# Graph output bias as a per-partition scalar of the self-feature sum, value copies on ScalarE, and another place for one group's condition features

## Chip, cores and metric

The kernel runs on one core of a Trainium2 chip. The time is the device time of one execution in microseconds. Before the change the median of three runs is 674.63 us (674.51 to 674.78).

A core has a matrix engine (TensorE, PE in the profile, with its weight loads listed as PEld), a vector engine (VectorE, DVE), an engine for activation functions and scaled copies (ScalarE, ACT), a general engine (GpSimd, POOL) and a queue that issues most transfers (SyncE, SP). Each executes its own instructions in order and waits on semaphores for the others. Transfers between HBM and the core's SBUF run on 16 DMA engines. PE writes to PSUM, which VectorE and ScalarE read; GpSimd works on SBUF alone.

## The reference, cut to what matters

64 batches of 64 tokens with 256 features. A graph attention over the first 20 tokens of each batch, in two directions with 16 heads, is followed by a transformer block with adaptive layer norms. The change touches only the graph attention. Cut to its core:

```python
row_zero = v.sum(-1) == 0
q_exp = where(row_zero[..., None], 0, q[:, None, :])
self_feat = concat([v, q_exp], -1) @ W_self.T + b_self
output = self_feat
for d in range(2):
    A = adj_f if d == 0 else swapaxes(adj_f, 1, 2)
    A = A[:, :, :20, :]
    cond = A.sum(-1);  vb = A @ w_bias + b_bias
    kv = self_feat[:, :20]
    aff = qh @ kh * 0.25                      # 16 heads
    aff = where(cond > 0, aff, NEG) + vb
    w = softmax(aff, -1)
    out = einsum('bnhf,hgf->bnhg', w @ kv, Wout[d]) + bout[d]
    output = output + out
x = v + relu(output)
# then: layer norm, 16-head attention, gated residual, layer norm, gelu MLP, gated residual
```

Since the softmax weights of a row sum to 1, adding `bout` to the values before the weighting gives the same sum as adding it to the output after it. Over the two directions the second form adds `bout[0] + bout[1]`, which depends on the feature alone.

## The kernel before, in words

**Layout.** Everything is kept transposed: features on the 128 partitions in two halves c = 0, 1, tokens along the free dimension. The batches are cut into nine groups (`NB`): group 0 of 4 batches (256 tokens), groups 1 to 7 of 8 batches (512 tokens), group 8 of 4. A tile is 128 tokens, two batches; a group has two or four tiles, numbered j.

**Order.** The schedule is written out by hand; each engine executes in the order in which the Python code emits. `start()` brings group 0 through the graph stage and prepares groups 1 and 2. Then for g = 1 to 7 come `boundary(g)` and `period(g)`; `finish()` does the rest. In a period each *slot* (`slot`, L763) works on one tile E of group g in the transformer block and one tile C of group g+1 in the graph stage: scores of both, `block_turned` and `graph_turned` for the tiles of the slot before (`Eb`, `Cb`), keys for the next slot, `block_exp(E)`, `graph_masked(C)`, `block_sums(E)`, `graph_exp(C)`, `block_weights(E)`, `block_attended(Eb)`, `graph_output` for each of `Cb`, `graph_normal(C)`. Between these stand named places ("p", "p2", "f0", "f1", "d0", "d0b", "f2", "f2a", "f2b", "d1", "d2", "f3") that `fill` fills with work of other groups: MLP products of group g-1 (`mlp_up` L735, `mlp_down` L745), features and masks of group g+2. `start()` ends with two slots for the tiles (0, 0), (0, 1) of the block and (1, 2), (1, 3) of the graph stage; the first of them has `Cb` = the tiles 0 and 1 of group 1 and the flag `late`, by which `graph_exp(C)` and `block_weights(E)` stand behind the two `graph_output`.

**PSUM.** `pair` gives the two score buffers "pa" and "pb"; `bank` hands out four others in rotation, so a product can only start when the reader of what last stood in its bank is done.

**Self features.** `self_product` (L324) multiplies x with W_self; `self_cond` makes `tq`, the conditioning masked by the rows that are not zero; `self_features` (L331) adds the product, `b_self` and `tq` on VectorE and GpSimd copies the first 20 tokens to `kv`. For groups 0 to 2 `self_cond` reads the row sums from PSUM on VectorE (L309). From group 3 on `nonzero_rows` sums the rows of x on VectorE (L288), compares (L291), and SP writes the 512 flags to DRAM (`nzd`, L293), element by element, and reads them back spread over the partitions (`nzb`, L294); `self_cond` is then a GpSimd product (L315), one for each half c. For group 3 `nonzero_rows` is called in `boundary(1)`, and both `self_cond` stand in "f1" of slot 0 of period 1, behind `graph_masked(C)`; for later groups they stand in "d2".

**Masks.** `load_adj` loads two tables of 440 KB into the two buffers `a_d`; `mask_step` reduces them on VectorE to `keep` and `term` (L347 to L360). The tables of group 3 are loaded in `boundary(1)` ahead of `nonzero_rows(3)` and read from slot 1 of period 1 on.

**Values.** `graph_v` multiplies `kv` with Wout (L371 for the first 128 rows, L382 for the other 32), adds the bias on VectorE into `v_sb` (L373 with `bout_sb`, L387 with `bout4`), and SP writes that to DRAM, from where `graph_v_spread` (L395) brings it into `vblk` in the form that `graph_output` needs. `bout_sb` and `bout4` are filled at the start by five broadcasting transfers (L149, L151) between the loads of wq and those of group 1.

**Scores to output.** `graph_masked`: VectorE multiplies the scores by `keep` (L469), GpSimd adds `term` (L474). `graph_exp`: VectorE takes the maximum (L479) and subtracts it (L480), ScalarE takes the exponent (L481). `graph_normal`: L486, L487 on VectorE, L488 on GpSimd. `graph_turned` transposes on PE (L496), copies on ScalarE (L500). `graph_output` multiplies with the values (L514) into `po`. For the tiles of group 0 and tiles 0 and 1 of group 1 (`early`) PE also adds the self features by an identity product (L510) and ScalarE takes the Relu out of PSUM (L521); for all others VectorE adds (L523) and ScalarE takes the Relu (L524). GpSimd adds the result to x (L525). Each fp32 product shows as two matmuls in the profile.

**Block stage.** `block_exp` (L629, L631 on VectorE, L635 on ScalarE), `block_sums` (L639), `block_weights` (L642 on VectorE, L643 on GpSimd), `block_turned` (L654 on PE, L657 on ScalarE), `block_attended` (L665, L675). ScalarE has to load an activation table between Exp and Gelu (the table loads under L635 and L737).

Of the kernel before, what the change touches and what calls it, by code (L numbers as in the profile page):

```python
# [9 lines left out]
F32 = mybir.dt.float32  # L10
I32 = mybir.dt.int32
AF = mybir.ActivationFunctionType
# [5 lines left out]
P = 128  # L18
# [15 lines left out]
_COLS = [  # L34
    ("b_self", 2), ("bq0", 2), ("bq1", 2), ("bk0", 2), ("bk1", 2),
    ("bq", 2), ("bk", 2), ("bv", 2), ("bproj", 2), ("b1", 8), ("b2", 2), ("bt", 12),
    ("g1", 2), ("be1", 2), ("g2", 2), ("be2", 2),
]
COL = {}
NCOL = 0  # L40
# [6 lines left out]
def graph_attention_then_dit_block(  # L47
# [11 lines left out]
    wq: bass.AP,  # L59
    wk: bass.AP,  # L60
    wout: bass.AP,
    bout: bass.AP,
    wqkv: bass.AP,
    wproj: bass.AP,
    w1: bass.AP,
# [77 lines left out]
    wk_sb = [load_w(f"wk{d}", wk[d], 2, D, nc.sync) for d in range(2)]  # L143
    load_adj(0)
    wq_sb = [load_w(f"wq{d}", wq[d], 2, D, nc.sync) for d in range(2)]
    bout_sb = const.tile([P, 2 * D], F32, name="bout_sb")

    bout4 = const.tile([P, P], F32, name="bout4")
    nc.sync.dma_start(bout_sb, bout.partition_broadcast(P))  # L149
    for i in range(4):  # L150
        nc.sync.dma_start(bout4[ts(i, 32), :], bout[ts(i, P)].partition_broadcast(32))  # L151
    load_xT(1)
    wout_sb = load_w("wout", wout, 2, 2 * D, nc.sync)
    wb = const.tile([P, L], F32, name="wb")
# [44 lines left out]
    nc.gpsimd.tensor_tensor(hmask2, hmask4[:, 0:2], hmask4[:, 2:4], ALU.add)  # L199
    mhalf = const.tile([P, 2], F32, name="mhalf")  # L200
    nc.gpsimd.memset(mhalf, -0.5)

    vblk = const.tile([4 * M, GB, 2, HD, 8], F32, name="vblk")

# [158 lines left out]
    def graph_v(g, part):  # L363

        G = groups[g]
        if part == 0:
            n = min(G.nb * M, P)
            G.vd = dram.tile([GB * M, 2 * D], F32, tag="vd", name="vd")[0 : G.nb * M, :]
            pv = bank("pv")[0:n, :]
            for k in range(2):  # L370
                nc.tensor.matmul(pv, G.kv[:, k, 0:n], wout_sb[:, k, :], start=(k == 0), stop=(k == 1))  # L371
            v_sb = small.tile([P, 2 * D], F32, tag="v_sb", name="v_sb", bufs=1)[0:n, :]
            nc.vector.tensor_tensor(v_sb, pv, bout_sb[0:n, :], ALU.add)  # L373
            nc.sync.dma_start(G.vd[0:n, :], v_sb)
            return
        if G.nb * M <= P:
            return

        pv = bank("pv4")
        for k in range(2):  # L380
            for i in range(4):
                nc.tensor.matmul(  # L382
                    pv[ts(i, 32), 0:P], G.kv[:, k, ds(P, 32)], wout_sb[:, k, ts(i, P)],
                    start=(k == 0), stop=(k == 1), tile_position=(0, 32 * i),
                )
        v4_sb = small.tile([P, P], F32, tag="v4_sb", name="v4_sb", bufs=1)
        nc.vector.tensor_tensor(v4_sb, pv[:, 0:P], bout4, ALU.add)  # L387
        for i in range(4):
            nc.sync.dma_start(G.vd[P : GB * M, ts(i, P)], v4_sb[ts(i, 32), :])

# [38 lines left out]
    def graph_keys(g, j):  # L429

        G = groups[g]
        G.kblk = getattr(G, "kblk", {})
        kblk = G.kblk[j] = two.tile([P, 2, 2, 2, 4 * M], F32, tag="kblk", name="kblk")
        if g == 1:
            for h in range(4):
                nc.scalar.activation(
                    kblk.rearrange("p d c s (h m) -> p h (d c s) m", h=4)[:, h],
                    G.kT[:, j].rearrange("p d c (s m) -> p (d c s) m", s=2), AF.Copy, scale=hmask4[:, h : h + 1],
                )
            return  # L440
        nc.gpsimd.tensor_tensor(
            kblk.rearrange("p d c s (h m) -> p (d c s) h m", h=4),
            G.kT[:, j].rearrange("p d c (s m) -> p (d c s) m", s=2).unsqueeze(2).to_broadcast([P, 8, 4, M]),
            hmask4.unsqueeze(1).unsqueeze(3).to_broadcast([P, 8, 4, M]), ALU.mult,
        )
# [56 lines left out]
    def graph_output(t, po):  # L502

        G, j = groups[t.g], t.j
        sf, xs = G.sfT[:, :, ts(j, P)], G.xT[:, :, ts(j, P)]
        po2 = po[:, 0:D].rearrange("p (c t) -> p c t", c=2)
        early = t.g == 0 or (t.g == 1 and j < 2)
        if early:
            for c in range(2):
                nc.tensor.matmul(po2[:, c], ident, sf[:, c], start=(c == 0), stop=False, skip_group_check=True)  # L510
        for c in range(2):
            for s in range(2):
                for i in range(4):
                    nc.tensor.matmul(  # L514
                        po[ts(i, 32), ds(c * P + s * N, N)],
                        vblk[:, 2 * j + s, :, :, 4 * c + i].rearrange("p h e -> p (h e)"),
                        t.wT[:, 4 * c + i, ts(s, N)], start=not early, stop=True, tile_position=(0, 32 * i),
                        skip_group_check=early,
                    )
        if early:  # L520
            nc.scalar.activation(sf, po2, AF.Relu)  # L521
        else:
            nc.vector.tensor_tensor(sf, po2, sf, ALU.add)  # L523
            nc.scalar.activation(sf, sf, AF.Relu)  # L524
        nc.gpsimd.tensor_tensor(xs, xs, sf, ALU.add)  # L525

# [236 lines left out]
    def slot(e, c, e_next, c_next, before, fill, late=False):  # L763
        Eb, Cb = before
        fill("p")
        sc = [pair("pa", "sca"), pair("pb", "scb")] if e or c else None
        E = block_scores(*e, sc) if e else None
        C = graph_scores(*c, sc) if c else None
        fill("p2")
        if Eb:  # L770
            block_turned(Eb)
        elif Cb:
            graph_turned(Cb[0])
        fill("f0")
        if e_next:
            block_keys(*e_next)
        if c_next and c_next[0] != 1:
            graph_keys(*c_next)
        if E:
            block_exp(E)  # L780
        if c_next and c_next[0] == 1:
            graph_keys(*c_next)
        if C:
            graph_masked(C)
        fill("f1")
        if Eb and Cb:
            graph_turned(Cb[0])
        if E:
            block_sums(E)
        fill("d0")  # L790
        if C and not late:
            graph_exp(C)
        fill("d0b")
        if E and not late:

            block_weights(E)
        if Eb:
            block_attended(Eb, pair("pa", "pao")[:, 0])
        fill("f2")
        for i, t in enumerate(Cb):  # L800
            if i > 0:
                graph_turned(t)
                fill("f2a")
            graph_output(t, pair("pa" if i > 0 else "pb", "po")[:, 0])
        if late:
            graph_exp(C)
            block_weights(E)
        fill("f2b")
        fill("d1")
        if C:  # L810
            graph_normal(C)
        fill("d2")
        fill("f3")
        return E, [C] if C else []

    def boundary(g, before):
# [36 lines left out]
        if a_on:  # L853
            if g > 1:
                load_x(g + 2)
            load_xT(g + 2)
            load_adj(g + 2)
        K = [Tile() for _ in range(A.nt // 2)]
        if g == NG - 2:
            pair_proj(g - 1, 0)  # L860
            norm_tokens(G, G.xT, 1)
            norm_stats(G)
            normed(G)
            pair_product(g - 1, 1)
            graph_q(g + 1, 1, 0)
            norm_tokens(K[0], A.xT, 0)
            pair_gated(g - 1, 1)
            modulated(G, G.hT, 1, amp1, off1, g)
            pair_added(g - 1, 1)
            graph_q(g + 1, 1, 1)  # L870
            graph_k(g + 1, 1)
            norm_stats(K[0])
        else:
            if Cb:
                norm_tokens(G, G.xT, 1)
                norm_stats(G)
            block_proj(g - 1, 0)
            if Cb:
                normed(G)
            block_proj(g - 1, 1)  # L880
            if c_on:
                graph_q(g + 1, 1, 0)
            if g == 1:
                graph_q(2, 1, 1)
            if Cb:
                modulated(G, G.hT, 1, amp1, off1, g)
            if not c_on:
                mlp_down(g - 2, 1, 4, 5)
            if c_on:
                graph_k(g + 1, 1)  # L890
            if g == 1:
                nonzero_rows(3)
            for j2, k in enumerate(K):
                norm_tokens(k, A.xT, j2)
                norm_stats(k)
# [59 lines left out]
    def period(g):  # L955
# [36 lines left out]
        else:  # L992
            fills = [
                {
                    "f1": [(block_v, g, i) for i in range(1 if g in (1, NG - 2) else 0, 2)] + (conds if g == 1 else []),
                    "d0": masks(0) if g > 1 else [],
                    "d2": masks(1) + conds if g > 1 else [],
                    "f3": up(0, 1, 2, 3),
# [34 lines left out]
    def start():  # L1033
# [74 lines left out]
        for t in t1:  # L1108
# [31 lines left out]
            },  # L1140
            {
                "f1": [(half_normed, 1, 1)],
                "d0b": [(half_normed, 1, 2), (graph_v, 2, 0)],
                "f2b": [(time_product, 4), (time_product, 5), (time_sum, 4), (time_sum, 5)],
            },
        ]
# [163 lines left out]
```

## Time and profile before

| what | value |
|---|---|
| median of 3 runs | 674.63 us |
| profiled execution, whole time | 675.26 us |
| its span, from the first to the last instruction | 673.6 us |
| TensorE clock granted | 1.00 throughout |
| busy: PE / PEld / DVE / ACT / POOL | 655.7 / 404.2 / 472.2 / 354.9 / 371.5 us |
| L373 and L387, the bias adds on the values | 9 of 683 ns and 7 of 282 ns |
| L523, the self-feature sum; L521, the Relu of the early tiles | 28 of 392 ns; 4 of 384 ns |
| L510, the identity products of the early tiles | 16 matmuls, 2.5 us busy |
| L315, condition features of groups 3 to 8 | 12, 12.0 us busy |
| DMA | 33.42 MB, q1 (SP) busy 15.2% of 16 engines' span |

Busy time is what an engine spent on instructions; PE's is modelled, since matmuls are pipelined. In the lists, an entry gives its start, its length, the engine, the line of the kernel, what it writes and reads, and in brackets how long the engine had idled before it and what it waited for. "SPq" is SP issuing a transfer; the transfer itself ends later. Busy times of some 97% for PE say that the other engines matter where PE waits for them.

### The profile page before, as it was taken

The page shows a single profiled execution, that of the slowest core. Times are in us where ns is not written, and L with a number is a line of the kernel's source. Part 1 is how long each engine was busy: PE and PEld are TensorE (multiplying, and loading weights), DVE is VectorE, ACT ScalarE, POOL GpSimd, SP SyncE. Part 2 cuts the span into 40 slices and gives each one's busy share as a digit, 9 for nine tenths or more (in the row PEclk, how much of TensorE's full clock was granted, in tenths as well). Part 3 has the DMA queues.
Part 4 walks back from the last instruction along what each step waited for, and adds up shares of the span by engine and source line. Part 5 has one row for each costly group of instructions (what it writes and reads, how often), then busy time and mean ns, then how long its engine had stood idle before and what let it go on. Part 6 is the DMA issues. An engine that isn't in the chain of part 4 may idle for free.

```text
span 673.6 us, 15450 instructions
## 1 busy us (share of the span) xinstructions
PE 655.7 (97%) x6422; PEld 404.2 (60%) x6422; DVE 472.2 (70%) x859; ACT 354.9 (53%) x627; POOL 371.5 (55%) x366
## 2 busy tenths in 40 slices
PE   8999898999999999999999999999999999999997
PEld 7657656775555565565555655555565675556546
DVE  4988967997777677776776777776777865656221
ACT  3364537763666337744476436654377444854412
POOL 5556557756664567653584555744667546445210
PEclk9999999999999999999999999999999999999999
DMA  7626030014100310004000140003000000000000
GB/s 239 201 87 209 27 99 18 18 34 123 18 1 34 126 31 17 18 17 156 1 18 18 36 137 17 2 32 89 10 10 11 18 26 1 2 18 1 17 16 32
DMA packets 34654, 33.42 MB, mean 50 GB/s; under 512 B 5624, under 2 KB 28408, under 8 KB 34584
## 3 DMA queue, kind: packets, MB, share of 16 engines
q1 hardware_dynamic: 34104, 32.33, 15.2%
q8 instruction: 51, 0.84, 0.6%
q14 instruction: 19, 0.16, 0.1%
q10 hardware_dynamic: 416, 0.09, 0.1%
q0 software_dynamic: 64, 0.01, 0.0%
HBM read 25.59 MB, written 6.83 MB: 48 GB/s over the span
## 4 chain that ended last, share of the span: by engine, by line
PE 84%; DVE 7%; ACT 3%; POOL 2%; issue 1%; DMA 1%; SPq 0%; ACTq 0%; POOLq 0%; DVEq 0%
PE py L745 15%; PE pu L735 15%; PE pqT L422 8%; PE pqk L580 8%; PE ppT L654 4%; PE pv L588 4%; PE pwT L496 3%; PE pf L324 3%; PE pproj L690 3%; PE po L514 3%; PE pk L407 2%; PE pao L665 2%; PE pv L371 2%; PE sca L618 2%; PE pxT L533 2%; PE phT L560 2%
## 5 line engine op out<-in xcount | busy, mean ns | idle before, releaser
L745 PE MATMUL py<-u,w 128*128 128x512 f32 (+1 forms) x272 | 117.9, 561 | 0.2 <-ACT u L737 0.2
L735 PE MATMUL pu<-h2T,w 128*128 128x512 f32 (+1 forms) x256 | 108.8, 569 | 0.9 <-POOL h2T L567 0.5
L643 POOL TENSOR_TENSOR pr<-pr,sm 128x1024 f32<-128x1024 f32 x32 | 60.9, 1903 | 69.0 <-DVE sm L642 48.3
L474 POOL TENSOR_TENSOR w<-w,term 128x640 f32<-128x640 f32 x32 | 49.5, 1550 | 72.4 <-DVE w L469 39.4
L735 PEld LDWEIGHTS pu<-h2T,w 128*128 128x128 f32 x256 | 47.7, 190 | 48.6 <-issue 43.0
L745 PEld LDWEIGHTS py<-u,w 128*128 128x128 f32 x272 | 47.8, 190 | 36.4 <-issue 32.9
L737 ACT ACTIVATE u<-pu,vec 128x512 f32<-128x512 f32 (+1 forms) x72 | 43.2, 640 | 34.3 <-PE pu L735 34.1
L422 PE MATMUL pqT<-sfT,wq 128*128 128x512 f32 (+1 forms) x144 | 60.7, 551 | 0.3 <-DVE y L713 0.3
L580 PE MATMUL pqk<-hT,wqkv 128*128 128x512 f32 (+1 forms) x144 | 59.8, 551 | 0.5 <-POOL hT L567 0.4
L629 DVE TENSOR_REDUCE mx<-sca 128x8 f32<-128x512 f32 x32 | 22.0, 689 | 50.4 <-PE sca L458 49.0
L639 DVE TENSOR_REDUCE sm<-pr 128x16 f32<-128x1024 f32 x32 | 38.9, 1217 | 21.6 <-ACT pr L635 21.3
L481 ACT ACTIVATE w<-w 128x640 f32<-128x640 f32 x32 | 23.5, 736 | 57.9 <-DVE w L480 57.9
L423 ACT ACTIVATE qT<-pqT,vec 128x512 f32<-128x512 f32 (+1 forms) x36 | 23.0, 640 | 50.9 <-PE pqT L422 50.6
L635 ACT ACTIVATE pr<-pr 128x1024 f32<-128x1024 f32 x32 | 33.8, 1057 | 26.9 <-DVE pr L631 26.6
L657 ACT COPY pT<-ppT 128x512 f32<-128x512 f32 x64 | 34.4, 591 | 25.1 <-PE ppT L654 25.1
L546 POOL TENSOR_TENSOR rstd<-rstd,mhalf 128x2 f32<-128x2 f32 x32 | 23.3, 728 | 42.1 <-DVE rstd L545 41.1
L581 ACT ACTIVATE qk<-pqk,vec 128x512 f32<-128x512 f32 (+1 forms) x36 | 23.0, 640 | 43.4 <-PE pqk L580 43.4
L488 POOL TENSOR_TENSOR w<-w,sm 128x640 f32<-128x640 f32 x32 | 44.1, 1381 | 1.9 <-DVE sm L487 1.8
L551 DVE TENSOR_SCALAR xn<-xn,mv,rstd 128x256 f32<-128x256 f32 x64 | 37.9, 633 | 9.8 <-POOL rstd L546 9.8
L542 DVE BATCH_NORM_STATS2 st<-xn 128x6 f32<-128x256 f32 x64 | 26.1, 408 | 25.5 <-ACT xn L535 25.5
L525 POOL TENSOR_TENSOR xT<-xT,sfT 128x256 f32<-128x256 f32 x32 | 23.4, 731 | 32.6 <-ACT sfT L524 27.2
L500 ACT COPY wT<-pwT 80x512 f32<-80x512 f32 x64 | 34.0, 582 | 13.0 <-PE pwT L496 13.0
(146 smaller groups left out, 1429.7 us busy)
## 6 DMA issues: line engine op xcount, KB each, us to landing
xT<-in_x_t SPq DMA_DIRECT2D x7, 512.0 KB
out<-xT SPq DMA_DIRECT2D x14, 256.0 KB
a_d<-in_adj SPq DMA_DIRECT2D x7, 440.0 KB
a_d<-in_adj_t SPq DMA_DIRECT2D x7, 440.0 KB
x_g<-in_x SPq DMA_DIRECT2D x5, 512.0 KB
vblk<-vd SPq DMA_DIRECT2D x28, 80.0 KB
w<-in_w SPq DMA_DIRECT2D x2, 1024.0 KB
vd<-v_sb SPq DMA_DIRECT2D x7, 256.0 KB
```

The lines of the kernel that those rows point to most:

```text
L422: nc.tensor.matmul(pq, wq_sb[d][:, k, ts(c, P)], G.sfT[:, k, :], start=(k == 0), stop=(k == 1))
L474: nc.gpsimd.tensor_tensor(t.w, t.w, G.term[:, :, j, :].unsqueeze(1).to_broadcast([P, H, 2, M]), ALU.add)
L488: nc.gpsimd.tensor_tensor(wf, wf, sm.unsqueeze(2).to_broadcast([P, 2 * H, M]), ALU.mult)
L500: nc.scalar.copy(t.wT[:, ts(q4, 4), :], pt[0 : 4 * M, :].rearrange("p (i t) -> p i t", i=4))
L551: nc.vector.tensor_scalar(key.xn[:, i, :], key.xn[:, i, :], key.mv[:, i, 0:1], key.rstd[:, i : i + 1], ALU.subtract, ALU.mult,)
L580: nc.tensor.matmul(pp, wqkv_sb[:, k, ds(i * D + c * P, P)], G.hT[:, k, 0 : G.T], start=(k == 0), stop=(k == 1))
L639: nc.vector.tensor_reduce(t.sm, t.pr, AX.X, ALU.add)
L643: nc.gpsimd.tensor_tensor(t.pr, t.pr, t.sm.unsqueeze(2).to_broadcast([P, H, N]), ALU.mult)
L657: nc.scalar.copy(t.pT[:, ts(q4, 4), :], pt.rearrange("p (i t) -> p i t", i=4))
L735: nc.tensor.matmul(pu, w1_sb[:, k, ts(m, P)], G.h2T[:, k, 0 : G.T], start=(k == 0), stop=(k == 1))
L737: nc.scalar.activation(G.u[m], pu, AF.Gelu, bias=col("b1", m))
L745: nc.tensor.matmul(G.py, w2_sb[:, m, ts(c, P)], G.u[m], start=(m == 0), stop=(m == 7))
```

## The change

- The two `bout` vectors join the table `vec` (four columns more). A GpSimd add makes `bo`, their sum, 128x2. `bout_sb`, `bout4` and their five transfers go.
- `graph_v` copies the values on ScalarE in place of the add on VectorE.
- `graph_output` works by halves c: VectorE adds product, `bo` and self features in one `scalar_tensor_tensor` of 128x128 for each half; the Relu is then taken as before. For `early` tiles ScalarE takes Relu with `bo` as its bias, also by halves.
- `early` holds for group 0 alone: tiles 0 and 1 of group 1 lose the identity products and are summed on VectorE.
- Both `self_cond(3)` move to a new place "k" in the slot, behind the keys of the next slot and ahead of `block_exp(E)` and `graph_masked(C)`.
- `load_adj(3)` moves behind `nonzero_rows(3)`.
- In the second slot of `start()` `graph_v(2, 0)` moves from "d0b", where it stood behind `graph_exp(C)` and `half_normed(1, 2)`, to "d0", ahead of both.

```diff
-    bout_sb = const.tile([P, 2 * D], F32, name="bout_sb")
-    bout4 = const.tile([P, P], F32, name="bout4")
-    nc.sync.dma_start(bout_sb, bout.partition_broadcast(P))
-    for i in range(4):
-        nc.sync.dma_start(bout4[ts(i, 32), :], bout[ts(i, P)].partition_broadcast(32))
...
+    bo = const.tile([P, 2], F32, name="bo")
+    nc.gpsimd.tensor_tensor(
+        bo, vec[:, COL["bo0"] : COL["bo0"] + 2], vec[:, COL["bo1"] : COL["bo1"] + 2], ALU.add
+    )
...
-            nc.vector.tensor_tensor(v_sb, pv, bout_sb[0:n, :], ALU.add)
+            nc.scalar.copy(v_sb, pv)
...
-        nc.vector.tensor_tensor(v4_sb, pv[:, 0:P], bout4, ALU.add)
+        nc.scalar.copy(v4_sb, pv[:, 0:P])
...
-        early = t.g == 0 or (t.g == 1 and j < 2)
+        early = t.g == 0
...
-        if early:
-            nc.scalar.activation(sf, po2, AF.Relu)
-        else:
-            nc.vector.tensor_tensor(sf, po2, sf, ALU.add)
+        for c in range(2):
+            b = bo[:, c : c + 1]
+            if early:
+                nc.scalar.activation(sf[:, c], po2[:, c], AF.Relu, bias=b)
+            else:
+                nc.vector.scalar_tensor_tensor(sf[:, c], po2[:, c], b, sf[:, c], ALU.add, ALU.add)
+        if not early:
             nc.scalar.activation(sf, sf, AF.Relu)
...
         if c_next and c_next[0] != 1:
             graph_keys(*c_next)
+        fill("k")
         if E:
             block_exp(E)
...
             load_xT(g + 2)
-            load_adj(g + 2)
+            if g > 1:
+                load_adj(g + 2)
...
             if g == 1:
                 nonzero_rows(3)
+                load_adj(3)
...
-                    "f1": [(block_v, g, i) for i in range(1 if g in (1, NG - 2) else 0, 2)] + (conds if g == 1 else []),
+                    "f1": [(block_v, g, i) for i in range(1 if g in (1, NG - 2) else 0, 2)],
+                    "k": conds if g == 1 else [],
...
                 "f1": [(half_normed, 1, 1)],
-                "d0b": [(half_normed, 1, 2), (graph_v, 2, 0)],
+                "d0": [(graph_v, 2, 0)],
+                "d0b": [(half_normed, 1, 2)],
```

## The prediction

> **What bounds the kernel now.** First the page: the chain of work that ended last, by engine, over a span of 673.6 us.
>
> ```profile
> PE 84%; DVE 7%; ACT 3%; POOL 2%; issue 1%; DMA 1%; SPq 0%; ACTq 0%; POOLq 0%; DVEq 0%
> ```
>
> TensorE carries 84% of the chain. Where it does not is read from busy time by stretch (length, then PE, PEld, DVE, ACT, POOL):
>
> ```profile
> 0.00:50.00 50.00, 45.59 (x424) 32.79 (x424) 38.28 (x65) 21.62 (x47) 27.15 (x37) 1.00 0.55 176
> 50.00:110.00 60.00, 56.72 (x670) 39.51 (x655) 47.04 (x90) 28.18 (x58) 33.10 (x34) 1.00 0.33 101
> 110.00:125.00 15.00, 12.68 (x188) 9.27 (x179) 12.84 (x22) 11.91 (x21) 12.32 (x14) 1.00 0.01 3
> ...
> 145.00:500.00 355.00, 354.92 (x3405) 204.53 (x3404) 261.03 (x465) 193.89 (x333) 209.53 (x202) 1.00 0.15 44
> ```
>
> From 145 to 500 us PE is idle 0.08 us: edits to VectorE and ScalarE there are paid only if they use up their slack. Before 125 us PE is idle 10.0 us (4.41 + 3.28 + 2.32), so the change has to be costed in that stretch. The longest hole lies around 111 us, in slot 0 of period 1, and the chain in order of time names its cause:
>
> ```profile
> 105.97 1.55 POOL w L474
> 107.55 0.83 DVE mx L479
> 108.40 0.84 DVE w L480
> ...
> 111.37 1.38 ACT u L737 x4
> 112.75 0.06 issue
> 112.81 1.09 ACT pT L657 x2
> 113.92 1.28 ACT L635
> 115.22 1.07 ACT pr L635
> ...
> 117.45 0.75 DVE sfT L331
> 118.24 1.98 PE pf L324 x4
> ```
>
> From the GpSimd add L474 (`graph_masked`) to PE's L324 every piece begins when the one before ends. There is no slack: a microsecond by which L474 is late is a microsecond for PE.
>
> Last, the DMA pair that `self_cond(3)` needs (SP's timeline) and GpSimd's timeline around it, with a later group's pair for comparison.
>
> ```profile
> 92.31 0.37 SPq L293 DMA_DIRECT2D nzd<-nz  x1
> 101.31 0.34 SPq L294 DMA_DIRECT2D nzb<-nzd  x1
> ```
>
> ```profile
> 100.93 1.25 POOL L441 TENSOR_TENSOR kblk<-kT,hmask 128x640 f32<-128x640 f32 x1
> 105.97 1.54 POOL L474 TENSOR_TENSOR w<-w,term 128x640 f32<-128x640 f32 x1 [3.79 <-DVE w L469]
> 107.47 2.66 POOL L315 TENSOR_TENSOR tq<-nzb,qwT 128x512 f32<-128x512 f32 x2
> 110.09 1.90 POOL L643 TENSOR_TENSOR pr<-pr,sm 128x1024 f32<-128x1024 f32 x1
> ```
>
> ```profile
> 420.15 2.04 POOL L315 TENSOR_TENSOR tq<-nzb,qwT 128x512 f32<-128x512 f32 x2 [1.06 <-DMA nzb<-nzd]
> ```
>
> GpSimd has a gap of 3.79 us from 102.18 to 105.97. The question is whether nzb is there in it.
>
> **The fourth group's cond (group index 3).** The two L315 move from behind L474 into that gap. They need nzb. Four later groups show GpSimd waiting for nzb, so its arrival is exact there, counted from SP's issue of nzd: 182.20 - 167.85 = 14.35, 261.21 - 246.95 = 14.26, 340.45 - 326.03 = 14.42, 420.15 - 405.11 = 15.04 us. For group 3 nzd is issued at 92.31, which gives 106.6 to 107.35; L315 found nzb there at 107.47, which agrees, and DMA moves nzb's bytes from 104.3 to 106.0. What comes before nzd (L288 and L291 behind L563 on VectorE, behind PE's transposes at 89.6) is not touched. So the gap closes before the data come. L315 x2 runs from 106.66 (by 14.35) for 2.05, its time in the groups where VectorE is not beside it, to 108.71; L474 starts at 108.75 instead of 105.97: **+2.8**. Bounds: nzb usable as its last byte is moved, 106.0 + 2.05 - 105.97 = +2.1; 15.04 and the 2.66 of this group, 107.35 + 2.66 - 105.97 = +4.0. Queued behind the waiting L315 are L474, then the weights L643; behind L474 VectorE's L479, L480, L642, behind these ScalarE's exponent L481, the Gelu's table load, four u and the pT copies. All shift by the same. What the move buys is that L643 no longer stands behind L315 (109.45 instead of 110.09), but pT is held by ScalarE until 112.75 anyway, so that is worth 0.
>
> [...]
>
> **The adj loads of group 3** move past nzd and nzb on SP: 880 KB issued after nzb, at about 101.7, not at 85.1. Before, xT and both tables took 5.7 us from first issue to last byte (84.66 to 90.4), so they land near 108; VectorE reads the first at 122.05: hidden with 14 us to spare. They may share the engines with nzb, though: bounds 0 (nzb is ahead) and its whole transfer again, +1.7. While nzb moves, the DMA engines are busy 62% (0.2 us windows from 104.3 to 106.1), so there is room: **+0.2**.
>
> **Values copied by ScalarE.** Nine L373 adds (683 ns) and seven L387 (282) leave VectorE; nine ScalarE copies (591, the row of L657, 128x512 from PSUM) and seven of about 0.3 (L675 with bias: 358) come. At 19.3 VectorE loses 0.69, but L479 at 19.99 waits for GpSimd's first L474 (18.41 to 19.94): 0. At 44.9 the copies fall into a ScalarE gap of 2.6 us and the next exponent stands behind PE's pqk: 0. In slot 1 of the start VectorE runs unbroken from 66.02 to L642 at 74.89, for which GpSimd's L643 and PE's ppT (idle 0.92) wait: -0.60 there. In period 1, slot 2, ScalarE runs unbroken from 130.34 to 138.9, and its second wT copy ends as PE starts po at 138.58 (0.80 instead of 0.68): the copy, 0.5 when back to back, comes ahead of the table load and puts off wT; PE's second half of po waits: **+0.4** (bounds 0 and 0.6). In later periods the wT copies end 1.6 us or more ahead of po (214.5 against 216.1), which covers it; without that cover it would be 0.5 in each of four periods.
>
> **The bias as a scalar, two tiles more.** Thirty tiles take two 128x128 adds instead of 28 one 128x256 (392 ns). The row is missing; bounds L254 (281) and L1239 (350), 0.22 from start to start when back to back (L254's pitch 0.20). The pair takes 0.5, its first half can begin on half the product; hidden from 145 us on by VectorE's waits for scores of 3.15 us. Tiles 0 and 1 of group 1 lose their identity products, 0.44 us of PE each. The first frees nothing: PE waits for L331 until 58.58. For the second: tile 0's sums come behind L309 (59.04), its Relu at 59.6, behind which ScalarE's wT copies end at 61.05 instead of 58.63; PE's po ends near 61.47 instead of 61.69. VectorE must wait for that before the exponent of the next tile: L479 at 61.74, not 59.04; as L486 waited for ScalarE until 62.79 anyway, only part is handed on: 61.74 + 0.84 + 0.82 + 0.77 for L481 brings L486 to 64.2, L347 to 65.3, L254 to 66.33, L629 to 66.55 instead of 66.02: +0.53. With the -0.60 from the value add, PE's ppT at 77.24 comes **0.1 earlier** (bounds -0.6 and +0.6). Group 0's Relu in halves: 0; the second half starts where the whole did.
>
> **The front.** Five SP issues (6.79 to 11.05) and 320 KB go, later loads come 4 us earlier. VectorE waits 0.50 for adj of group 0 at 10.75; traffic behind it changes: between -0.5 and +0.4, taken as 0, since as much is queued in its place. The bo add (some 0.2, as L199) lies in GpSimd's idle 4.4 to 9.38; four columns more in vec: 0.
>
> **Sum.** 2.8 + 0.2 + 0.4 - 0.1 = +3.3. The profiled execution took 675.26 (1.66 around its span) and would take 678.6; it lies 0.63 above the median of 674.63, so the median goes to **677.9**.
>
> **Rivals.** (1) nzb is in time: usable by 103.9 (105.97 - 2.05), L474 keeps its place, and 674.63 + 0.4 - 0.1 = 674.9. For it speaks that the DMA engines are empty from 93.6 to 104.3 and that the adj loads no longer precede nzd; against it that those were done at 90.4 and that groups without a load near have the same 14.3. It takes the loss away from 103.9 down, and by equal steps in between. (2) The adj loads collide with nzb: 2.8 + 1.7 + 0.4 - 0.1, 679.4; for it the issue within 1 us of nzb, against it nzb's place ahead. (3) As (1), and the front is freed too: 0.50 at 10.75, 0.44 for the second identity product if VectorE is not late there, 0.60 at 75, and no loss at 138: 674.63 - 1.54 = 673.1. Against it: VectorE's wait for po in slot 0.
>
> **Chances.** Forecast 0.68, rivals 0.14, 0.08, 0.10. The forecast's own range is 676.5 to 679.6; to leave out 2 in 10 at most the range reaches down to the first rival: 674.8 to 679.6. About 0.2% (1.35 us) can be told from no change; faster 0.09, within 0.17, slower 0.74.
>
> **What will show it.** In the changed profile: L315 with a wait on nzb ahead of L474 in period 1; L474 some 2.8 us later after the first scores than now; PE's hole before ppT there near 3.9 instead of 1.87 us; no new hole from 150 to 500 us; L629 of the second start slot some 0.5 later after slot 0, ppT about even. If L315 starts at 102.2 and L474 follows VectorE without delay, the forecast is wrong by its largest term.

## The result, and the profile after

| kernel | median of runs | profiled execution | its span |
|---|---|---|---|
| before, beside it | 674.72 us (674.51 to 675.68, 6 runs) | 675.26 us | 673.6 us |
| changed | 680.81 us (678.90 to 681.08, 6 runs) | 681.04 us | 679.3 us |

The ratio is 1.0072 (95%: 1.0052 to 1.0092): the change costs some 0.7%. (The two medians of the table, set against each other, give 1.0090, inside the same interval.) Applied to 674.63 us the ratio gives 679.5 us, just below the end of the predicted range; the median itself lies 1.2 us above that end. The sign was right. The size was short: 3.3 us were predicted, 4.9 us (by the ratio) to 6.1 us (by the medians) were measured.

The chain of waits of the changed kernel, by engine: PE's share has fallen from 84% to 81%, DVE, POOL and DMA have grown.

```profile
PE 81%; DVE 9%; ACT 3%; POOL 3%; issue 2%; DMA 2%; SPq 0%; ACTq 0%; POOLq 0%; DVEq 0%
```

Busy time by stretch, changed kernel, same stretches and columns as before the change (after the five engines stands the granted clock):

```profile
0.00:50.00 50.00, 46.40 (x436) 33.28 (x440) 37.30 (x64) 23.84 (x52) 27.71 (x38) 1.00 0.54 170
50.00:110.00 60.00, 55.82 (x627) 37.93 (x622) 45.74 (x89) 27.88 (x58) 31.84 (x33) 1.00 0.33 100
110.00:125.00 15.00, 10.60 (x124) 7.34 (x116) 10.22 (x18) 9.25 (x15) 8.65 (x9) 0.77 0.01 2
...
145.00:500.00 355.00, 354.92 (x3376) 205.47 (x3369) 260.30 (x479) 194.75 (x341) 210.84 (x198) 1.00 0.14 44
```

From 145 to 500 us PE is as busy as before. The third row carries the loss: PE is idle 4.40 us there instead of 2.32, and the clock column, 1.00 before, says 0.77. GpSimd and SP in that stretch:

```profile
106.91 2.05 POOL L313 TENSOR_TENSOR tq<-nzb,qwT 128x512 f32<-128x512 f32 x2 [4.38 <-DMA nzb<-nzd]
108.91 1.54 POOL L472 TENSOR_TENSOR w<-w,term 128x640 f32<-128x640 f32 x1
```

```profile
92.65 0.38 SPq L291 DMA_DIRECT2D nzd<-nz  x1
102.77 0.34 SPq L292 DMA_DIRECT2D nzb<-nzd  x1
```

L313 (L315 before) now waits in the gap for nzb and gets it 106.91 - 92.65 = 14.26 us after nzd was issued; L472 (L474 before) runs behind it, at 108.91 instead of 105.97. Next PE, before the change and after it (pu is the product before the hole, ppT the one behind it):

```profile
107.71 1.13 PE L735 MATMUL pu<-h2T,w 128*128 128x256 f32 x4 [0.43 <-ACT v L595]
112.05 1.09 PE L654 MATMUL ppT<-ident,pr 128*128 128x128 f32 x8 [1.87 <-POOL pr L643]
112.97 1.03 PE L745 MATMUL py<-u,w 128*128 128x256 f32 x4
113.84 1.88 PE L324 MATMUL pf<-xT,w_self 128*128 128x512 f32 x4
118.24 1.98 PE L324 MATMUL pf<-xT,w_self 128*128 128x512 f32 x4 [0.45 <-DVE sfT L331]
```

```profile
108.06 1.13 PE L736 MATMUL pu<-h2T,w 128*128 128x256 f32 x4 [0.44 <-ACT v L596]
114.93 1.94 PE L655 MATMUL ppT<-ident,pr 128*128 128x128 f32 x8 [4.40 <-ACT u L738]
116.66 1.91 PE L746 MATMUL py<-u,w 128*128 128x256 f32 x4
118.37 3.09 PE L322 MATMUL pf<-xT,w_self 128*128 128x512 f32 x4
123.46 1.98 PE L322 MATMUL pf<-xT,w_self 128*128 128x512 f32 x4
```

The same eight products of ppT take 1.94 us instead of 1.09, the four of py 1.91 instead of 1.03. Windows of 1 us of the changed kernel name the reason, in the clock column:

```profile
113.00:114.00 1.00, 0.00 (x0) 0.00 (x0) 0.94 (x2) 0.99 (x1) 1.00 (x1) 0.98 0.00 0
114.00:115.00 1.00, 0.07 (x1) 0.10 (x2) 1.00 (x3) 0.99 (x3) 0.99 (x2) 0.50 0.00 0
...
120.00:121.00 1.00, 1.00 (x3) 0.46 (x2) 1.00 (x1) 0.00 (x0) 0.00 (x0) 0.60 0.00 0
121.00:122.00 1.00, 1.00 (x9) 0.70 (x7) 0.62 (x2) 0.07 (x1) 0.00 (x0) 1.00 0.00 0
```

A mean of 0.98 in the first and 0.60 in the third of these puts the half clock at 113.96 to 120.80 us. So the wait is paid twice: once as idle time, 4.40 us instead of 1.87 in front of ppT, once as slow products behind it, for 6.84 us at half clock. The runs below have shorter holes there, and behind one of 2.48 us the clock fell too.

By landmarks, the changed kernel stands behind the old one by -0.41 us at pf in slot 0 of the start (58.17 against 58.58), +0.27 at the next slot's ppT (77.51), +0.34 at nzd (92.65), +2.94 at L472 (108.91), +5.22 at the second pf of period 1 (123.46), +5.55 at the next nzd (173.40) and +5.79 at the end. What is added from L472 to pf, 2.28 us, has no term in the prediction.

Medians of the old kernel in the sets of runs below are 675.2 to 675.6 us, where its runs fall into those with a mean granted clock of 1.00 (medians of 674.4 to 674.9 us) and of 0.997 (675.7 to 676.0 us); the changed kernel's have 0.995 five times and 0.997 once, and that one is the 678.90.

### The profile page after: what moved, and what is told of

Same layout as the page of the kernel before. It is cut to its first block, busy times and chain, and to the rows that moved or that the text cites. A ratio compares the mean times of both kernels' runs of the same rounds, so it can differ in the third digit from the quotient of the medians.

```text
span 679.3 us, 15485 instructions
## 1 busy us (share of the span) xinstructions
PE 659.1 (97%) x6414; PEld 405.1 (60%) x6414; DVE 469.4 (69%) x875; ACT 361.9 (53%) x645; POOL 375.1 (55%) x367
## 4 chain that ended last, share of the span: by engine, by line
PE 81%; DVE 9%; ACT 3%; POOL 3%; issue 2%; DMA 2%; SPq 0%; ACTq 0%; POOLq 0%; DVEq 0%
PE py L746 15%; PE pu L736 14%; PE pqT L420 8%; PE pqk L581 7%; PE ppT L655 4%; PE pwT L494 3%; PE pv L589 3%; PE pf L322 3%; PE pproj L691 3%; PE po L512 3%; PE pao L666 2%; PE phT L561 2%; PE pxT L534 2%; PE pk L405 2%; PE sca L619 2%
## 5 line engine op out<-in xcount | busy, mean ns | idle before, releaser
L472 POOL TENSOR_TENSOR w<-w,term 128x640 f32<-128x640 f32 x32 | 49.4, 1547 | 68.5 <-DVE w L467 40.1
L630 DVE TENSOR_REDUCE mx<-sca 128x8 f32<-128x512 f32 x32 | 22.0, 688 | 48.7 <-PE sca L456 47.3
L655 PE MATMUL ppT<-ident,pr 128*128 128x128 f32 x256 | 36.1, 284 | 7.0 <-ACT u L738 4.9
```

The costliest lines, as they stand in the source:

```text
L472: nc.gpsimd.tensor_tensor(t.w, t.w, G.term[:, :, j, :].unsqueeze(1).to_broadcast([P, H, 2, M]), ALU.add)
L655: nc.tensor.transpose(pt[:, ts(i, P)], t.pr[:, ts(q4 * 4 + i, 2), :].rearrange("p h m -> p (h m)"), ident)
```

## Which part costs the time

**The conds alone, and the change without them.** Two complementary kernels: the change with the two conds in their old place, and the old kernel with only the conds (and the loads of the adjacency block) moved.

```diff
 # e1: the changed kernel
-                    "f1": [(block_v, g, i) ...],
-                    "k": conds if g == 1 else [],
+                    "f1": [(block_v, g, i) ...] + (conds if g == 1 else []),
 # e2: the kernel before
-                    "f1": [(block_v, g, i) ...] + (conds if g == 1 else []),
+                    "f1": [(block_v, g, i) ...],
+                    "k": conds if g == 1 else [],
+        fill("k")     # ahead of block_exp(E); load_adj(3) behind nonzero_rows(3)
```

> The changed kernel with the two condition products of group 3 back behind the GpSimd add of the masks (their place before the change); everything else as changed, the later adj loads too. Theory: the late nzb is what holds the add, and the long hole that follows drops PE's clock; with the products back the hole of 4.4 us becomes about 1.9, the clock stays 1.00, and some 4.9 us (2.6 for the add, 2.3 for the clock) come back: about 675.5 us where the changed kernel has 680.8. What is left over the kernel before, some 0.7 us, is then the tiles summed on VectorE and the copies on ScalarE, less the front. Rival (the sums and the copies are what costs): above 678.

> The kernel before with only the two condition products of group 3 moved ahead of the mask add and the adj loads of group 3 moved behind the flags. Theory: the products wait for nzb until 14.3 us after nzd is issued, the add comes 2.6 us late, PE idles over 4 us and its clock falls to half for some 6 us: about 679.5 us, clock 0.995. Rival (the loss needs the other parts of the change): below 677.

Measured: with the conds back 677.01 us, ratio 1.0027 (1.0015 to 1.0038), the hole 1.88 us again and the clock 1.00 from 50 to 500 us. The conds alone 680.37 us, ratio 1.0075 (1.0060 to 1.0091). GpSimd and PE of the kernel with the conds alone:

```profile
107.78 2.04 POOL L315 TENSOR_TENSOR tq<-nzb,qwT 128x512 f32<-128x512 f32 x2 [5.12 <-DMA nzb<-nzd]
```

```profile
115.80 1.94 PE L654 MATMUL ppT<-ident,pr 128*128 128x128 f32 x8 [5.15 <-ACT u L737]
```

nzd was issued at 92.78 there, so nzb took 15.00 us, and ppT took the 1.94 us of the half clock. The move of the conds is the large loss by itself; the rest of the change costs 0.27%. The 677.01 us lie 1.5 us above what was expected of the first kernel. The two losses do not simply add up to that of the change: by the profiled executions they are 0.79 and 5.68 us, 6.47 in all, against 5.78; in the kernel with the conds alone nzb took 0.74 us longer than in the changed one.

**Only nzb's arrival counts (e4).** In the changed kernel the flags of group 3 are made one step earlier, behind boundary 1's mask steps, one of which moves behind the graph output; the conds stay in the gap.

```diff
-            for i in {1: (3, 1, 2, 4), 2: (1, 2, 4)}.get(g, (4, 5, 6)):
+            for i in {1: (3, 1, 2), 2: (1, 2, 4)}.get(g, (4, 5, 6)):
                 mask_step(g + 1, i)
+            if g == 1:
+                nonzero_rows(3)
...
+            if g == 1:
+                mask_step(2, 4)
...
             if g == 1:
-                nonzero_rows(3)
                 load_adj(3)
```

> The changed kernel with the flags of group 3 made some 9 us earlier: the row sums, the comparison and the two transfers stand in the mask steps of group 2 in boundary 1, and one mask step goes behind the graph output. The products stay in their new place. Theory (only the arrival of nzb counts): nzb is usable near 97 us, the products run in GpSimd's gap at about 102.5, the mask add follows VectorE without delay, the hole is under 2 us, clock 1.00: 675.5 to 676.3, some 0.4 of it for row sums that now stand ahead of the layer norm's statistics. Rival (the order of the products ahead of the add costs in itself): above 678.

Measured: 677.14 us, ratio 1.0029 (1.0018 to 1.0040), the time of the kernel with the conds back, though 0.8 us above the upper end of what was expected. nzd was issued at 82.88, and GpSimd shows no wait on nzb:

```profile
102.94 2.04 POOL L313 TENSOR_TENSOR tq<-nzb,qwT 128x512 f32<-128x512 f32 x2
106.78 1.55 POOL L472 TENSOR_TENSOR w<-w,term 128x640 f32<-128x640 f32 x1 [1.80 <-DVE w L467]
```

L472 follows VectorE again, ppT waits 1.83 us, the clock is 1.00. The place in the gap is harmless once the data are there, but it gains nothing either: ScalarE sets the time, as the prediction had it (ppT waits for ScalarE's u, as it does in the changed kernel).

**The adjacency loads beside nzb (e5).** The changed kernel with the loads of group 3 ahead of the flags again.

```diff
-            if g > 1:
-                load_adj(g + 2)
+            load_adj(g + 2)
...
                 nonzero_rows(3)
-                load_adj(3)
```

> The changed kernel with the loads of the next group's adjacency block back ahead of the flags and their round trip through HBM. My theory: nzb is usable 14.3 us after nzd is issued either way, so the products of the fourth group's cond wait as long, the hole before ppT is 4.4 us and the whole stays at 680.8 within 0.3. [...]

Measured: 680.84 us, ratio 1.0070 (1.0058 to 1.0082): no difference to the changed kernel. nzd at 93.98, L313 at 108.13: 14.15 us. The kernels that load behind the flags show 14.00 to 15.00 us (14.26 in the changed kernel, 15.00 with the conds alone, 14.05, 14.28 and 14.00 in the three of the next section), so no price of a collision can be told from the scatter; the 0.2 that was added is not shown.

The profile of this kernel shows something else. Its hole is nearly as long as that of the changed kernel, but the clock was halved for 3.42 us only, from 116.58 to 120.00 us:

```profile
116.14 1.54 PE L655 MATMUL ppT<-ident,pr 128*128 128x128 f32 x8 [4.30 <-ACT u L738]
123.48 1.98 PE L322 MATMUL pf<-xT,w_self 128*128 128x512 f32 x4
```

From L472 (110.13) to the second pf it takes 13.35 us, against 14.55 in the changed kernel and 12.27 before the change: 1.08 us for the half clock instead of 2.28.

## Is the clock worth 2.3 us?

Extra products whose result nobody reads fill part of PE's wait: 14 (e3), then 8 (e3b), then 12 (e9).

```diff
+    def keep_busy(n):
+        for _ in range(n):
+            nc.tensor.matmul(last["sc"][0][:, 1, 416:512], ones, w_self_sb[:, 0, 0:96], start=True, stop=True)
...
+                    "p2": [(keep_busy, 14)] if g == 1 else [],
```

> The changed kernel with 14 products of 96 columns more on PE, results unused, issued right behind the scores of slot 1 of period 1, where PE otherwise idles 4.4 us. They end before VectorE reads those scores. Theory (half clock because of the idle time): the granted clock stays 1.00, the products behind the hole run at their usual speed, and the time falls by about 2.3 us to some 678.5 in spite of the extra work. Rival (the clock has nothing to do with this hole, or its fall is hidden): 680.8 or more.

> The changed kernel, with 8 extra products of 96 columns (into a part of the scores' bank that nobody reads) behind the scores of slot 1 of period 1, in place of the 14 of the earlier run. At about 0.24 us each they fill some 1.95 us of the 4.40 us in which TensorE waits before ppT. Clock theory (the wait costs twice: the conds come late, and the idle time then halves TensorE's clock for some 6 us): the wait left is about 2.5 us, the granted clock stays 1.00 from 106 to 128 us, ppT starts where it did (6.9 us after pu), from pu to the second pf it is about 13 us instead of 15.4, and the whole is 2.3 us below the changed kernel, near 678.4, if the products displace nothing later. Rival (the clock halves but the matmuls had slack there): clock 1.00, but pu to pf stays at 15.4 and the whole at 680.8. With 14 products a copy of v by ScalarE at 185 us waited for a pu group and cost 1.3 us there; if that comes back with 8 it belongs to the extra instructions, and the whole is near 679.7.

> The changed kernel with 12 extra products behind the scores of slot 1 of period 1 (8 left a wait of 2.5 us, and the clock still fell to half for 3.5 us instead of 6.6; 14 kept it at 1.00, but a copy of v at 185 us was late then). Clock theory: 12 fill some 2.9 us, the wait left is 1.5 us, less than the 1.87 that the kernel before has at full clock, so the clock stays 1.00 and from pu to the second pf it is about 13 us; if nothing is late at 185 us, the whole is 2.4 us below the changed kernel, near 678.4, a ratio of about 1.0045, and the run's mean clock is one or two steps of 0.0025 higher. If the copy at 185 is late again: near 679.7. If half clock costs nothing: 680.8.

| extra products | wait before ppT | half clock | pu to second pf | median | ratio |
|---|---|---|---|---|---|
| 0 (changed kernel) | 4.40 us | 113.96 to 120.80 | 15.40 us | 680.81 | 1.0072 (1.0052 to 1.0092) |
| 8 | 2.48 us | 115.88 to 119.28 | 14.24 us | 679.92 | 1.0063 (1.0051 to 1.0075) |
| 12 | 1.31 us | none | 12.87 us | 680.32 | 1.0071 (1.0053 to 1.0089) |
| 14 | 0.90 us | none there | 12.92 us | 680.86 | 1.0089 (1.0072 to 1.0107) |

PE of the kernel with 12 extra products:

```profile
107.86 1.13 PE L736 MATMUL pu<-h2T,w 128*128 128x256 f32 x4 [0.43 <-ACT v L596]
114.48 1.06 PE L655 MATMUL ppT<-ident,pr 128*128 128x128 f32 x8 [1.31 <-ACT u L738]
120.73 1.98 PE L322 MATMUL pf<-xT,w_self 128*128 128x512 f32 x4 [0.47 <-DVE sfT L329]
```

Locally the theory holds. With the clock up, the stretch of 12.87 us exceeds the old kernel's 10.53 us (107.71 to 118.24) by 2.34 us. That is the conds' delay alone: L472 starts 0.60 us behind pu (108.46), where L474 started 1.74 us ahead of it (105.97). With 14 products both numbers are 2.39 us. In the changed kernel they are 4.87 and 2.59, so 2.28 us are the clock's; the rest of the 2.5 us by which the stretch is shorter comes from nzb, which was there 0.2 to 0.3 us sooner after nzd. The whole did not follow as expected. For 8 products the expectation of a full clock failed: behind a hole of 2.48 us the clock stood at half from 115.88 to 119.28 us. The rows are PE's and 1-us windows of that kernel:

```profile
110.68 2.02 PE L768 MATMUL sca<-w_self,ones 128*128 128x96 f32 x16
115.19 1.30 PE L655 MATMUL ppT<-ident,pr 128*128 128x128 f32 x8 [2.48 <-ACT u L738]
```

```profile
115.00:116.00 1.00, 0.81 (x7) 0.84 (x8) 1.00 (x3) 1.00 (x4) 1.00 (x2) 0.94 0.00 0
116.00:117.00 1.00, 1.00 (x5) 0.91 (x4) 1.00 (x3) 1.00 (x3) 1.00 (x2) 0.50 0.00 0
118.00:119.00 1.00, 1.00 (x3) 0.48 (x2) 0.00 (x0) 0.99 (x2) 1.00 (x2) 0.50 0.00 0
119.00:120.00 1.00, 1.00 (x4) 0.45 (x3) 0.49 (x1) 0.48 (x1) 0.77 (x1) 0.86 0.00 0
```

With 12 and 14 products a copy of v by ScalarE was late near 181 and 185 us. ScalarE of the kernel with 12:

```profile
176.47 1.48 ACT L596 COPY v<-pv 64x256 f32<-64x256 f32 x4
181.27 1.50 ACT L596 COPY v<-pv 64x256 f32<-64x256 f32 x4 [3.31 <-PE pu L736]
```

In the changed kernel the two halves ran back to back (179.21, 3.02 us). Up to there the saving is whole: the second nzd comes 2.74 us earlier than in the changed kernel (170.66 against 173.40), of which the front had 0.20. Behind the late copy, for which PE waits 0.82 us, some 1.1 us of that are gone, and the last transfers start 1.68 us earlier (673.15 against 674.83); that execution took 679.38 us. The medians show even less, since three of the six runs with 12 had a mean clock of 0.997 (680.92 to 681.43) and three of 1.00 (679.38 to 679.72). The profile with 14 lost its front to a half clock from 9.16 to 12.56 us, behind a late w_self, for which PE had waited 1.62 us. So the 2.5 us are shown in the stretch and for 60 us behind it, not in the medians. Why 12 and 14 extra products, but not 8, put off a copy 70 us later stays open.

## The start: two tiles' sums and the copies

Four kernels, all with the conds in their old place, cross the two parts that the prediction netted to -0.1: sums of tiles 0 and 1 of group 1 on VectorE or as before, values copied by ScalarE or VectorE.

```diff
 # e6 and e11: the two tiles as before
-        early = t.g == 0
+        early = t.g == 0 or (t.g == 1 and j < 2)
 # e7 and e11: copies on VectorE
-            nc.scalar.copy(v_sb, pv)
+            nc.vector.tensor_copy(v_sb, pv)
...
-        nc.scalar.copy(v4_sb, pv[:, 0:P])
+        nc.vector.tensor_copy(v4_sb, pv[:, 0:P])
```

> The changed kernel with the conds back in their old place, and tiles 0 and 1 of the second group summed as before the change (TensorE adds the features, ScalarE reads the sum). Theory (the two sums on VectorE stand ahead of the second half of the softmax in the second start slot, wait 2.0 us for the graph output there, and take 0.6 each): the maximum over w starts near 59 us instead of 61.7, pr is divided about 0.6 earlier, ppT near 76.8 instead of 77.4, and the whole is 0.5 to 0.9 below that of the kernel with the conds put back, near 676.3. Rival (the copy of the values by ScalarE is what is late there): no change, 677.0.

> The changed kernel with the conds back in their old place, and the copies of the values (v_sb and v4) on VectorE again. By the prediction's terms: 0.6 us more in the second start slot (75.0 us, where PE waited 0.87 for the copy in the kernel before) and 0.4 less in the second slot of period 1 (138 us), so 0.2 more in all, near 677.2. Rival (the copy gains nothing in the start slot, since the graph sums stand before it on VectorE and set the time): 0.4 less, near 676.6.

> The changed kernel with the conds in their old place, tiles 0 and 1 of the second group summed as before, and the values copied by VectorE: of the change only the bias as a scalar of the sums (and the later loads of the adjacency block) is left. Theory (the two costs are separate, 1.2 for the two tiles, 0.6 for the copy): from the second start slot's pf to ppT 18.65 us as in the kernel before, 0.2 to 0.4 lost in period 1, the whole near 675.3 (ratio about 1.0005). Rival (the copy only counts because the two sums made VectorE late): 18.05, and the whole near 674.7.

| kernel | sums of the two tiles | copies | pf to ppT in the start | whole | ratio |
|---|---|---|---|---|---|
| before | PE and ScalarE | VectorE (add) | 18.66 us | | |
| conds back (e1) | VectorE | ScalarE | 19.34 us | 677.01 | 1.0027 (1.0015 to 1.0038) |
| e6 | PE and ScalarE | ScalarE | 18.05 us | 674.98 | 1.0000 (0.9984 to 1.0017) |
| e7 | VectorE | VectorE | 19.92 us | 677.63 | 1.0034 (1.0022 to 1.0047) |
| e11 | PE and ScalarE | VectorE | 18.67 us | 676.61 | 1.0010 (0.9998 to 1.0022) |

Pf is the one of slot 0 (58.08 in e1), ppT the one of slot 1 (77.42). The two costs are separate: the copies gain 0.58 and 0.62 us, as predicted, and the sums cost 1.29 and 1.25 where 0.53 were predicted. The whole times go the same way, though they miss what was expected of e6, e7 and e11 (676.3, 677.2 and 675.3 us) by 0.4 to 1.3 us. VectorE in slot 0, before the change and after it:

```profile
59.04 0.81 DVE L479 TENSOR_REDUCE mx<-w 128x32 f32<-128x640 f32 x1
59.88 0.82 DVE L480 TENSOR_TENSOR w<-w,mx 128x640 f32<-128x640 f32 x1
...
62.79 0.82 DVE L486 TENSOR_REDUCE sm<-w 128x32 f32<-128x640 f32 x1 [1.34 <-ACT w L481]
...
66.02 0.69 DVE L629 TENSOR_REDUCE mx<-sca 128x8 f32<-128x512 f32 x1 [0.80 <-PE sca L458]
```

```profile
61.24 0.61 DVE L523 SCALAR_TENSOR_TENSOR sfT<-po,bo,sfT 128x128 f32<-128x128 f32 x2 [2.01 <-PE po L512]
61.77 0.81 DVE L477 TENSOR_REDUCE mx<-w 128x32 f32<-128x640 f32 x1
62.61 1.18 DVE L478 TENSOR_TENSOR w<-w,mx 128x640 f32<-128x640 f32 x1
...
66.89 0.68 DVE L630 TENSOR_REDUCE mx<-sca 128x8 f32<-128x512 f32 x1
```

VectorE stands 2.01 us in front of the sum for po, with the next tile's maximum ready behind it (58.65 us in e6). The prediction had that queue and the start of L477 (61.74, 61.33 with the front's 0.41); it came at 61.77, and L478 took 1.18 us instead of 0.82, beside GpSimd's add of the second tile (L526, 62.38 to 63.11 us), which came only after VectorE's pass before the change; in the kernel before, the same pass took 1.29 us where it ran beside GpSimd's L474 (20.84 us). That this is the cause was not tested. With the 1.18 us VectorE's slack ahead of L630 (0.80 before) was gone, and L630 came 0.75 us later than predicted for this front.

In e11 the profile caught another half clock, from 76.74 to 80.16 us, behind two short holes of PE; from ppT to pqk that execution takes 16.64 us instead of 14.96 in e6.

```profile
75.09 0.66 PE L561 MATMUL phT<-ident,xn 128*128 128x128 f32 x4 [1.10 <-DVE tp L252]
76.50 1.79 PE L655 MATMUL ppT<-ident,pr 128*128 128x128 f32 x8 [0.76 <-POOL pr L644]
```

The +0.4 that the prediction charged to the copies in slot 2 of period 1 is there, but mostly not theirs: from pqk to the next nzd the old kernel takes 75.73 us, e11 (bias as a scalar, and the later loads) 75.95, e6 and e1 (copies on ScalarE too) 76.05 and 76.06. So the sums with the bias, costed at nothing, take some 0.2 us, and the copies 0.1. The second kernel of the next section agrees: it leaves the loads and these copies as they were, sums only the third group in the new form, and takes 75.97.

## Versions that keep what is good

The first (e12) mends both losses: flags early as in e4, the two tiles as before as in e6. The second (e10) is the old kernel with the new form (copy on ScalarE, bias in the sum) for the third group alone, whose copy is the one that pays.

```diff
 # e10: the kernel before
-            nc.vector.tensor_tensor(v_sb, pv, bout_sb[0:n, :], ALU.add)
+            if g == 2:
+                nc.scalar.copy(v_sb, pv)
+            else:
+                nc.vector.tensor_tensor(v_sb, pv, bout_sb[0:n, :], ALU.add)
...
+        elif t.g == 2:
+            for c in range(2):
+                nc.vector.scalar_tensor_tensor(sf[:, c], po2[:, c], bo[:, c : c + 1], sf[:, c], ALU.add, ALU.add)
+            nc.scalar.activation(sf, sf, AF.Relu)
```

> The changed kernel with both of its losses mended: the fourth group's flags made one boundary earlier, so that nzb is there when the conds come to the gap, and tiles 0 and 1 of the second group summed as before. Theory: no wait on nzb, ppT in period 1 as in the kernel before, clock 1.00, and the whole like that of the kernel with conds back and the two tiles as before, ratio 1.000 (674.9). Rival (the earlier flags put 1 to 2 us on VectorE where PE waits for it): ratio 1.002.

> The kernel before, with the new form of the values (copied by ScalarE, bias added as the scalar of VectorE's sum) for the third group alone, whose copy stands in slot 1 of the start. Theory: the copy takes 0.6 off VectorE's unbroken run there and nothing else changes: from pf (58.58) to ppT (77.24) 18.05 us instead of 18.66, and the whole 0.6 below the kernel before (ratio 0.9990). Rival (what the third group's sums cost VectorE in period 1 takes it back: the kernels with the bias as a scalar lose 0.35 to 0.4 between 130 and 168 us): ratio 0.9995 to 1.0.

Measured: 675.63 us for the first, ratio 1.0009 (0.9992 to 1.0026), no loss left that can be told from none. 674.55 us for the second, ratio 0.9986 (0.9973 to 0.9998), the only kernel whose interval lies below the old one; its profiled execution took 673.96 us. PE of the second:

```profile
57.68 1.98 PE L329 MATMUL pf<-xT,w_self 128*128 128x512 f32 x4 [0.62 <-DVE sfT L336]
...
75.71 1.09 PE L669 MATMUL ppT<-ident,pr 128*128 128x128 f32 x8 [0.32 <-POOL pr L658]
```

From pf to ppT 18.03 us (18.05 expected, 18.66 before); the third group's sums give back 0.24 us of the 0.63 by the next nzd (90.85 us behind ppT instead of 90.61). That leaves 0.4 us; the rest of the 1.0 us by the medians is within their interval. (Among runs with a mean clock of 1.00 the two medians are 674.25 and 674.91 us, 0.7 apart.) This kernel has `graph_v(2, 0)` in its old place, and its 18.03 us are e6's 18.05: that move, for which the prediction has no term, is worth nothing that shows here.

## Why the prediction was right, and where it was short

- **nzb arrives too late for the gap**: right. 14.26 us against the rows' 14.26 to 15.04, L313 waiting ahead of L472. Of L472's 2.94 us, 0.34 were there at nzd, so the move cost 2.60 where 2.8 were predicted.
- **Everything behind L472 shifts by the same**: this step failed. The prediction had a hole of 3.9 us and priced it as idle time alone. It came out at 4.40, since ppT waited for ScalarE's u and not for the weights, and TensorE's clock was halved for 6.84 us behind it; 2.28 us of the 5.79 are that. The prediction shows the clock of 1.00 in its rows and has no term for its falling, though it lengthens the longest hole of the kernel.
- **The range**: that the 679.5 us lie in it is luck. The room above the forecast was given for other things, such as a later nzb (+4.0) or a collision of the loads (+1.7). Neither came, and the half clock filled it.
- **Adjacency loads, +0.2**: not shown; with the loads in either place nzb's time lies within the same scatter.
- **Copies, -0.60 in the start**: right (0.58 and 0.62). **+0.4 in period 1**: right in sum (0.33 from the second pf to the next nzd, 5.55 - 5.22), wrong in place; the bias sums carry most of it.
- **Two tiles, +0.53**: right mechanism, mis-sized, 1.25 to 1.29: the next tile's maximum started 0.44 us later than predicted for this front, and L478 took 0.36 longer. So ppT came 0.27 late instead of 0.1 early, though the front brought -0.41 where 0 was taken; the profiled fronts differ by more than that from one execution to another (pf at 57.68 us in e10, at 59.50 in e5).
- **No new hole from 145 to 500**: right, 354.92 us of PE in both; 0.24 us came by small steps behind the next nzd.

The profiled executions add up: 3.3 predicted; 2.28 for the clock, 0.44 for the start (0.34 at nzd instead of -0.1), -0.40 for the conds and loads (2.60 instead of 3.0), -0.07 in period 1 and 0.24 later make 5.79, which was measured. The 0.44 holds a front of -0.41 that may belong to this pair of executions alone.

## What to carry to other kernels

A wait that lengthens a hole of the matrix engine can have two prices: the hole, and the clock behind it, here 4.40 us of idle time and 2.28 us of slow products. Look up the longest hole and its place before moving anything in front of it, and ask how long it will be afterwards. Ahead of an in-order engine's critical instruction put only work whose data have arrived: the conds that waited for nzb put L472 off by 2.60 us, the place in the gap was harmless with the flags one step earlier, and two sums that stand in front of a ready maximum and wait for a product cost 1.25 us or more, where the prediction had 0.53.

## What the hardware showed beyond that

- The spells of half clock inside the profiled spans lasted 6.84 us (changed kernel), 6.82 (conds alone), 3.42 (e5), 3.40 (8 products), 3.42 (e11) and 3.40 (14 products, at the front). Behind nearly the same hole it was 6.84 us in the changed kernel (4.40 us) and 3.42 in e5 (4.30).
- How long a hole has to be for that, the runs don't settle. The clock fell behind 2.48 us with 8 products, behind 1.62 us at the front with 14, and behind 1.10 and 0.76 us close together in e11. It stayed at 1.00 behind 1.87 us in the old kernel and 1.88 in e1, behind 1.96 us at the front with the conds alone, and behind 1.09 and 0.76 us in e7, at the place of e11's two.
- A spell of 3.40 or 3.42 us cost 1.1 us (e5, and with 8 products 3.71 us over the old kernel's stretch where the conds' delay is 2.63) to 1.7 us (e11: 16.64 against 14.96). That is close to the step between the old kernel's runs at 1.00 (medians of 674.4 to 674.9 us) and at 0.997 (675.7 to 676.0); that it is the cause of that scatter was not shown, since no profile of the old kernel caught one.
